# Turning the second norm's tiles of the first two sequences through DRAM instead of on TensorE

## The chip, the cores and the metric

One core of a Trainium2 chip runs the whole program. The metric is device microseconds of one launch, the median of several runs; a profiled execution comes with a trace of every engine.

## The reference

The input `x` holds 4 sequences of 512 tokens, 512 wide. A layer of gated linear attention and a layer of a gated MLP are added to it, each behind a layer norm:

```
x = x + attention(layernorm(x))     # 4 heads of 128, chunks of 128 tokens, a running state per head
x = x + ffn(layernorm(x))           # gate and up 512 -> 4096, gelu(gate)*up, down 4096 -> 512

# attention, per sequence b, chunk n, head h
q, k, v = x@Wq + bq, x@Wk + bk, x@Wv + bv ;  k = k / |k|
cla     = cumsum(log(sigmoid(x@Walpha + balpha) + 1e-6))        # along the chunk
attn    = (q k^T) * beta * exp(cla_i - cla_j), lower triangle
y       = attn v + exp(cla) * (q state) ;  state = state * exp(cla_end) + v^T (k beta exp(cla_end - cla))
```

The MLP's weights are 4-bit codes with a scale for every 32 of them, unpacked on the chip. All is float32; the MLP's products are made of three parts (high, low, middle) of each number.

## The kernel before

The first phase is cut into 48 *places*, `p` from 0 to 47: 12 for each of the four sequences `b`, namely four V products, four Q products and four K products (`product_v`, `product_q`, `product_k`), each one [128 x 512]. The MLP follows, in rounds over weight tiles, and its first rounds are woven into the last places. All instructions are in the order in which the program writes them (a manual schedule): each engine has one queue in that order, and all transfers are issued by SP, on one queue.

`behind(p)` writes what goes behind product `p`. The chunks of attention follow the products at a distance. Chunk `c = 4b + n` (chunk n of sequence b) takes three places:

- place 9 + 3c: `chunk_lead`, `chunk_decay` (`dm` from the row sums `sums`, L608 on ScalarE, L612 on GpSimd);
- place 10 + 3c: `chunk_scores` (scores `sp`, L663; `dm` multiplied by them on VectorE, L674);
- place 11 + 3c: `chunk_sums` (`yp` from `dm`, L717 and L719; added to the residual `xr`, L726; stored as `acc`, L727), and then `second_norm`, the norm that feeds the MLP.

`norm` takes statistics of a tile (L334 to L341) and leaves `settle`, which writes the normalised tile `hn`. There are two ways to turn `hn` so that the model dimension lies on the partitions:

- on TensorE: `hn` goes on the list `turned`, and `turn` transposes it, four 128 x 128 blocks against the identity (L380), into a PSUM bank; `use` reads that bank;
- through DRAM, where `norm` gets a `way`: `settle` writes `hn` in a crossed order of columns (L349, two instructions), `cross` stores the tile (L310, 256 KB) and two places later loads it back in four transfers of 64 KB (L315), and three places after that `turn_blocks` turns its 32 x 32 blocks on VectorE (L326).

In the kernel before, the second way serves the first norm of sequences 1 to 3 (`way_a`, 12 tiles) and some tiles of k (`way_k`, 6 tiles). The first norm's tiles that take it are written at places 11, 14, ..., 32 for sequences 2 and 3; the tiles of sequence 1 earlier. The second norm's 16 tiles (`hn_f`) are turned on TensorE, two places behind their norm. `use` then makes the three parts `hi`, `lo`, `mi` (L406 on ScalarE, L407 and L408 on VectorE) and stores them to DRAM, three transfers of 256 KB (L410, `h<-g`), where the MLP's rounds load them (`x<-h`).

Two lists of postponed work hang on the places: `first_of[p]` is done at the beginning of `behind(p)`, `last_of[p]` at its end. Some loads are tied to places too. `load_sums(b, 0)` (L579), which brings the first chunk's row sums of a sequence from the little table `rows` (L563), is written at place 12b + 7 behind the calls of `turn`, two places ahead of the `chunk_decay` that reads it. Of each further chunk they are loaded three places ahead.

SBUF tiles of 2 KB a partition come from a list of free homes (`one_k`), first in, first out.

Of the kernel before, what the change touches and what calls it, by code (L numbers as in the profile page):

```python
# [21 lines left out]
P = 128  # L22
# [13 lines left out]
def f32(t):  # L36
    return t.bitcast(F32)
# [3 lines left out]
def tile_gated_linear_attention__then__nvfp4_geglu(  # L41
# [19 lines left out]
    nc = tc.nc  # L61
# [15 lines left out]
    h2d = [  # L77
        [dram.tile([KC, P, T], F32, tag=f"h2_{b}_{j}", name=f"h2_{b}_{j}") for j in range(3)]
        for b in range(B)
    ]  # L80
# [40 lines left out]
    one_k = Homes("b", 42, [P, T], two_k)  # L121
# [4 lines left out]
    def heads(t):  # L126
        return t.rearrange("p (h d) -> p h d", d=P)
# [170 lines left out]
    first_of, last_of = {}, {}  # L298
# [5 lines left out]
    def crossed(t):  # L304
        return t.rearrange("p (w k i) -> p k w i", w=KC, i=32)

    def cross(src, key, use, landing, turning):

        way = dram.tile([KC, P, P], F32, tag=f"way_{key}", name=f"way_{key}")
        nc.sync.dma_start(way.rearrange("w p m -> p w m"), f32(src).rearrange("p (w m) -> p w m", m=P))  # L310

        def land():
            t = one_k.get(f"way_{key}")
            for a in range(KC):
                nc.sync.dma_start(f32(t)[:, a * P : (a + 1) * P], way[:, a * 32 : (a + 1) * 32, :])  # L315
            last_of.setdefault(turning, []).append(lambda: use(t))

        first_of.setdefault(landing, []).append(land)

    def turn_blocks(t, *to):  # L320

        new = f32(t).rearrange("p (a k i) -> p k a i", a=KC, i=32)
        done = 0
        for part in to:
            n = part.shape[1]
            nc.vector.transpose(part.rearrange("p k (a j) -> p k a j", j=32), new[:, done : done + n])  # L326
            done += n
        one_k.put(t)

    def norm(src, key, use, parts=1, within=None, way=None):  # L330


        st = small.tile([P, 6], F32, tag="st", name=f"st_{key}")
        nc.vector.bn_stats(st, f32(src))  # L334
        if within:
            within()
        mv = small.tile([P, 2], F32, tag="mv", name=f"mv_{key}")
        nc.vector.bn_aggr(mv, st)
        rs = small.tile([P, 1], F32, tag="rs", name=f"rs_{key}")
        nc.vector.tensor_scalar(rs, mv[:, 1:2], 1e-5, None, ALU.add)  # L340
        nc.gpsimd.tensor_tensor(rs, rs, minus_half[:, :1], ALU.pow)  # L341

        def settle():

            hn = one_k.get(f"hn_{key}")
            w = D // parts
            if way:
                for c in range(2):
                    nc.vector.tensor_scalar(  # L349
                        crossed(f32(hn)).rearrange("p (c two) w i -> p c two w i", c=2)[:, c],  # L350
                        f32(src).rearrange("p (c w i two) -> p c two w i", c=2, w=KC, two=2)[:, c],
                        mv[:, 0:1], rs, ALU.subtract, ALU.mult,
                    )
                one_k.put(src)
                cross(hn, key, way, place[0] + 1, place[0] + 4)
                one_k.put(hn)
                return
            for cols in (slice(i * w, (i + 1) * w) for i in range(parts)):
                nc.vector.tensor_scalar(
                    f32(hn)[:, cols].rearrange("p (c two j) -> p c two j", two=2, j=P),  # L360
                    f32(src)[:, cols].rearrange("p (c j two) -> p c two j", two=2, j=P),
                    mv[:, 0:1], rs, ALU.subtract, ALU.mult,
                )
            one_k.put(src)
            turned.append((hn, key, use))

        settled.append(settle)
# [34 lines left out]
    def second_norm(b, n, src):  # L402
        def use(tp):
            g = [one_k.get(f"g{j}_{b}_{n}") for j in range(3)]
            hi, lo, mi = g
            nc.scalar.activation(hi, tp, AF.Copy, scale=HI)  # L406
            nc.vector.tensor_tensor(lo, tp, f32(hi), ALU.subtract)  # L407
            nc.vector.scalar_tensor_tensor(mi, f32(hi), ONE_E, tp, ALU.mult, ALU.subtract)  # L408
            for j in range(3):
                nc.sync.dma_start(  # L410
                    h2d[b][j][:, :, n * P : (n + 1) * P].rearrange("k p t -> p k t"), heads(f32(g[j]))
                )
            one_k.put(*g)

        norm(src, f"f{b}_{n}", use)


    zs, ss = {}, {}
# [289 lines left out]
    def chunk_sums(b, n):  # L708
        add = state_sums(b, n) if b < B - 1 else None
        old = ch.pop("old")  # L710
        one_k.put(v_sb.pop((b, n)))
        dm, vb = ch.pop("dm"), ch.pop("vb")
        qc = ch.pop("qc", None)
        yp = psum(f"yp_{b}_{n}")
        for h in range(H):
            hs = slice(h * P, (h + 1) * P)
            nc.tensor.matmul(yp[:, hs], f32(dm)[:, hs], f32(vb)[:, hs], start=True, stop=(n == 0))  # L717
            if n > 0:
                nc.tensor.matmul(yp[:, hs], f32(qc)[:, hs], f32(old)[:, hs], start=False, stop=True)  # L719
        one_k.put(dm, vb)  # L720
        if n > 0:
            one_k.put(qc, old)
        a = acc.pop((b, n))

        def sums():
            nc.vector.tensor_tensor(f32(a), f32(a), yp, ALU.add)  # L726
            nc.sync.dma_start(accd[b * NCH + n], f32(a))  # L727

        def rest():
            if n + 1 < NCH:  # L730
                chunk_values(b, n + 1)
            second_norm(b, n, a)
            if add:
                add()

        return sums, rest
# [3 lines left out]
    for b in range(1, B):  # L740
        for n in range(NCH):
            p = 3 * NCH * (b - 1) + 3 * n - 1 if b > 1 else 2 + 3 * max(n - 1, 0)
# [3 lines left out]
    place, met, summed = [0], set(), []  # L746
# [250 lines left out]
    with tc.manual_schedule():  # L997
# [45 lines left out]
        p = 0  # L1043
# [95 lines left out]
```

## Time and profile before

| | |
|---|---|
| median of 3 runs | 1303.22 us (1302.1 to 1303.25) |
| the profiled execution's own time | 1301.6 us |
| its span, first to last instruction | 1299.9 us |
| TensorE (PE) busy | 1288.6 us, 99% |
| VectorE (DVE) busy | 968.1 us, 74% |
| ScalarE (ACT) busy | 452.2 us, 35% |
| GpSimd (POOL) busy | 113.5 us, 9% |
| SP's DMA queue, share of 16 engines | 59.3% |
| granted TensorE clock, mean | 0.998 |

PE is the matmul side of TensorE, PEld its weight loads, SPq the queue on which SP issues transfers. A line of the timeline gives the start in us from the span's start, the time in us, the engine, the source line, the operation, output and inputs by the program's names, and in brackets how long the engine had been idle and what ended that. Names like `way_a` stand for all buffers of that name.

### The profile page before, as it was taken

The numbers are of one execution on the slowest core, as the hardware profiler recorded it, in microseconds if no ns is written. First come the engines' busy times: TensorE is split into PE (matmuls) and PEld (weight loads), VectorE is DVE, ScalarE is ACT, GpSimd is POOL, SyncE is SP. The second block draws the span as 40 slices with busy tenths as digits, with TensorE's granted clock in tenths as the row PEclk, the third lists the DMA queues.
The fourth block names the chain that finished last, engine by engine and source line by source line (L and its number), as shares of the span: only waits on it lengthen the run. The fifth ranks groups of instructions, "written<-read, shape, count | busy, mean of one in ns | idle before, by whom it ended". The sixth has DMA issues, their size and how long they took to land.

```text
span 1299.9 us, 17044 instructions
## 1 busy us (share of the span) xinstructions
PE 1288.6 (99%) x5736; PEld 1030.6 (79%) x5736; DVE 968.1 (74%) x1581; ACT 452.2 (35%) x878; POOL 113.5 (9%) x179
## 2 busy tenths in 40 slices
PE   9999999999999999999999999999999999999998
PEld 6667576778888888888888888888888888887886
DVE  4577865877777777777777777777777777777566
ACT  2333335743333333333333333333333333332332
POOL 1526462400000000000000000000000000000000
PEclk9999999999999999999999999999999999999999
DMA  6556667976565656555555565656555555555473
GB/s 208 163 163 191 196 191 226 310 263 213 179 195 178 194 178 194 178 195 178 194 178 194 178 194 179 195 178 194 179 194 179 192 181 190 182 179 199 167 253 126
DMA packets 195383, 250.24 MB, mean 193 GB/s; under 512 B 16672, under 2 KB 93792, under 8 KB 195296
## 3 DMA queue, kind: packets, MB, share of 16 engines
q1 hardware_dynamic: 195296, 249.16, 59.3%
q8 instruction: 45, 0.74, 0.2%
q14 instruction: 42, 0.34, 0.1%
HBM read 191.91 MB, written 57.18 MB: 192 GB/s over the span
## 4 chain that ended last, share of the span: by engine, by line
PE 95%; DVE 2%; DMA 1%; ACT 1%; issue 0%; SPq 0%; POOL 0%; DVEq 0%; ACTq 0%; POOLq 0%
PE pa L853 35%; PE p_d L897 26%; PE pb L853 18%; PE pq L450 4%; PE pk L474 3%; PE pva L425 2%; PE pvb L432 2%; PE yp L717 1%; PE sp L663 1%; PE yp L719 1%; PE dp L688 1%; PE tp_f L380 0%; DMA sums<-rows 0%; DMA acc<-acc 0%; DMA x<-h 0%
## 5 line engine op out<-in xcount | busy, mean ns | idle before, releaser
L853 PE MATMUL pa<-x,wgu 128*128 128x512 f32 x2048 | 508.5, 390 | 0.1
L853 PEld LDWEIGHTS pa<-x,wgu 128*128 128x128 f32 x2048 | 384.7, 188 | 80.0 <-DVE acc L909 0.4
L897 PE MATMUL p_d<-wd,i 128*128 128x512 f32 x1542 | 357.3, 389 | 2.3 <-DVE xr L726 0.6
L897 PEld LDWEIGHTS p_d<-wd,i 128*128 128x128 f32 x1542 | 288.2, 188 | 65.8 <-DVE i L877 2.1
L858 ACT ACTIVATE t<-pb 128x512 f32<-128x512 f32 x256 | 151.2, 591 | 357.9 <-PE pb L853 354.0
L853 PE MATMUL pb<-x,wgu 128*128 128x512 f32 x1024 | 273.7, 389 | 0.0
L859 DVE TENSOR_TENSOR t<-pa,t 128x512 f32<-128x512 f32 x256 | 176.4, 689 | 81.7 <-ACT t L858 76.4
L853 PEld LDWEIGHTS pb<-x,wgu 128*128 128x128 f32 x1024 | 192.3, 188 | 40.2
L905 DVE SCALAR_TENSOR_TENSOR acc<-p_d,acc 128x512 f32<-128x512 f32 (+1 forms) x137 | 93.3, 681 | 127.4 <-PE p_d L897 124.0
L873 ACT ACTIVATE i<-t 128x512 fp32r<-128x512 f32 x128 | 81.1, 634 | 194.2 <-DVE t L870 191.1
L865 ACT ACTIVATE t<-t 128x512 f32<-128x512 f32 x128 | 81.1, 634 | 136.0 <-DVE t L859 136.0
L877 DVE TENSOR_TENSOR i<-t,i 128x512 fp32r<-128x512 f32 x128 | 88.3, 690 | 26.0 <-ACT i L873 24.2
L909 DVE TENSOR_TENSOR acc<-acc,p_d 128x512 f32<-128x512 f32 x135 | 92.8, 688 | 14.4 <-PE p_d L897 0.5
L870 DVE SCALAR_TENSOR_TENSOR t<-t,t 128x512 f32<-128x512 f32 x128 | 88.6, 692 | 4.3
L928 POOL TENSOR_TENSOR acc<-acc,last 128x512 f32<-128x512 f32 x1 | 1.3, 1295 | 1015.1 <-ACT last L927 1015.1
L878 DVE SCALAR_TENSOR_TENSOR i<-i,t 128x512 fp32r<-128x512 f32 x128 | 88.9, 694 | 0.0
L450 PE MATMUL pq<-hT,wq 128*128 128x512 f32 x128 | 57.6, 595 | 0.0
L474 PE MATMUL pk<-wk,hT 128*128 128x512 f32 x128 | 57.4, 592 | 0.0
L450 PEld LDWEIGHTS pq<-hT,wq 128*128 128x128 f32 x128 | 23.6, 190 | 24.1 <-issue 23.9
L474 PEld LDWEIGHTS pk<-wk,hT 128*128 128x128 f32 x128 | 23.2, 190 | 23.9 <-issue 23.9
L183 DVE TENSOR_TENSOR wgu<-wgu,wgu 128x1024 fp32r<-128x1024 f32 x32 | 38.9, 1215 | 0.0
L180 DVE SCALAR_TENSOR_TENSOR wgu<-wgu,w_gu 128x1024 fp32r<-128x1024 f32 x32 | 38.9, 1215 | 0.0
(120 smaller groups left out, 901.6 us busy)
## 6 DMA issues: line engine op xcount, KB each, us to landing
x<-h SPq DMA_DIRECT2D x420, 256.0 KB
acc<-acc SPq DMA_DIRECT2D x256, 256.0 KB
h<-g SPq DMA_DIRECT2D x48, 256.0 KB
x<-in_x SPq DMA_DIRECT2D x16, 256.0 KB
pk_gu<-in_gate_p SPq DMA_DIRECT2D x32, 128.0 KB
sc_gu<-in_gate_s SPq DMA_DIRECT2D x64, 64.0 KB
pk_gu<-in_up_p SPq DMA_DIRECT2D x32, 128.0 KB
sc_gu<-in_up_s SPq DMA_DIRECT2D x64, 64.0 KB
```

What stands on the lines that cost most here:

```text
L450: nc.tensor.matmul(pq, f32(wq[k // 2])[:, k % 2, h * P : (h + 1) * P], f32(hT[b][k // 2])[:, k % 2, :], start=(k == 0), stop=(k == KC - 1),)
L474: nc.tensor.matmul(pk, f32(hT[b][k // 2])[:, k % 2, n * P : (n + 1) * P], f32(wk[k // 2])[:, k % 2, :], start=(k == 0), stop=(k == KC - 1),)
L853: nc.tensor.matmul(o, w3[j][:, k % 2, c * P : (c + 1) * P], x[j * KC + k], start=(j == js[0] and k == 0), stop=(j == js[-1] and k == KC - 1),)
L858: nc.scalar.activation(f32(t), pb, AF.Copy, scale=-1.0 / ONE_E)
L859: nc.vector.tensor_tensor(f32(t), pa, f32(t), ALU.add)
L865: nc.scalar.activation(f32(g), f32(g), AF.Gelu_apprx_tanh, scale=ONE_E)
L870: nc.vector.scalar_tensor_tensor(f32(u), f32(g), ONE_E, f32(u), ALU.mult, ALU.mult)
L877: nc.vector.tensor_tensor(il, f32(u), f32(ih), ALU.subtract)
L878: nc.vector.scalar_tensor_tensor(im, f32(ih), ONE_E, f32(u), ALU.mult, ALU.subtract)
L897: nc.tensor.matmul(banks[key_][:, part], inter[i][j][:, n * P : (n + 1) * P], wd[ms[i] // 2][j][:, ms[i] % 2, part], start=(i == 0 and j i ...
L905: nc.vector.scalar_tensor_tensor(a, banks[n, False, part.start][:, part], ONE_E, a, ALU.mult, ALU.add)
L909: nc.vector.tensor_tensor(a, a, banks[n, True, 0], ALU.subtract)
```

## The change

Eight of the second norm's 16 tiles, those of sequences 0 and 1, get a `way`: they are stored crossed, loaded back, turned in 32 x 32 blocks on VectorE into a new tile `h2T` in SBUF, and split into `hi`, `lo`, `mi` from there. For tile c that is: store at place 11 + 3c, loads at 13 + 3c, turn and split at the end of place 16 + 3c (it was in the middle of 13 + 3c). The three stores to `h2d` are made at the beginning of place 17 + 3c. Tiles of sequences 2 and 3 stay as they were.

```
@@ -406,13 +406,27 @@
             nc.scalar.activation(hi, tp, AF.Copy, scale=HI)
             nc.vector.tensor_tensor(lo, tp, f32(hi), ALU.subtract)
             nc.vector.scalar_tensor_tensor(mi, f32(hi), ONE_E, tp, ALU.mult, ALU.subtract)
-            for j in range(3):
-                nc.sync.dma_start(
-                    h2d[b][j][:, :, n * P : (n + 1) * P].rearrange("k p t -> p k t"), heads(f32(g[j]))
-                )
-            one_k.put(*g)
-
-        norm(src, f"f{b}_{n}", use)
+
+            def store():
+                for j in range(3):
+                    nc.sync.dma_start(
+                        h2d[b][j][:, :, n * P : (n + 1) * P].rearrange("k p t -> p k t"), heads(f32(g[j]))
+                    )
+                one_k.put(*g)
+
+
+            if b < 2:
+                first_of.setdefault(place[0], []).append(store)
+            else:
+                store()
+
+        def way(t):
+            whole = one_k.get(f"h2T_{b}_{n}")
+            turn_blocks(t, heads(f32(whole)))
+            use(f32(whole))
+            one_k.put(whole)
+
+        norm(src, f"f{b}_{n}", use, way=way if b < 2 else None)
```

## The prediction

> **What bounds the kernel now.** I read the page first, for the engine that is full, then the chain that ended last.
>
> ```profile
> PE 1288.6 (99%) x5736; PEld 1030.6 (79%) x5736; DVE 968.1 (74%) x1581; ACT 452.2 (35%) x878; POOL 113.5 (9%) x179
> PE 95%; DVE 2%; DMA 1%; ACT 1%; issue 0%; SPq 0%; POOL 0%; DVEq 0%; ACTq 0%; POOLq 0%
> ```
>
> TensorE is never idle, so whatever is taken off it is time gained, as long as nothing that it waits for comes late. So next its timeline in the attention phase:
>
> ```profile
> 105.25 0.60 PE L380 MATMUL tp_f<-ident,hn_f 128*128 128x128 f32 x4
> 105.68 1.06 PE L663 MATMUL sp<-q,kT 128*128 128x128 f32 x8
> ...
> 168.87 1.16 PE L717 MATMUL yp<-vb,dm 128*128 128x128 f32 x8 [0.21 <-DVE dm L674]
> ...
> 263.62 0.66 PE L593 MATMUL tpk<-ident,k 128*128 128x128 f32 x4 [2.57 <-DVE acc L905]
> 264.41 3.68 PE L853 MATMUL pa<-x,wgu 128*128 128x512 f32 x8
> ```
>
> The four transposes of a tile take 0.43 us from start to start. Only two waits stand in this phase. At 168.87 `yp` of chunk (2,0), sequence 2's first, waited for `dm`. The gap of 2.57 us was followed by 3.4 us at half clock: the `pa` behind it took 3.68 us where others take 2.0.
>
> The third view is what stands behind that `dm`, on SP, ScalarE and VectorE:
>
> ```profile
> 153.54 2.25 SPq L315 DMA_DIRECT2D way_a<-way_a  x4
> 155.89 2.75 SPq L410 DMA_DIRECT2D h<-g  x3
> 158.73 0.69 SPq L579 DMA_DIRECT2D sums<-rows  x1
> ...
> 163.98 1.28 ACT L608 ACTIVATE dm<-sums,ncla 128x128 f32<-128x128 f32 x4 [3.73 <-DMA sums<-rows]
> ...
> 168.14 0.68 DVE L674 TENSOR_TENSOR dm<-sp,dm 128x512 f32<-128x512 f32 x1
> ```
>
> The chunk's row sums are issued only behind the turned tile's four loads, ScalarE stands 3.73 us for them, and `dm` ends as TensorE wants it. So SP's queue is next to the path. It is late already: the transposes of place 25 ran at 119.25, and that place's `h<-g` were issued at 128.23.
>
> Last, how full the DMA is, with the windows view (the last but one column is the share of 16 engines):
>
> ```profile
> 68.00:69.00 1.00, 1.00 (x11) 1.00 (x11) 0.00 (x0) 0.05 (x1) 0.00 (x0) 1.00 0.30 89
> 70.00:71.00 1.00, 1.00 (x6) 0.84 (x6) 0.93 (x3) 0.00 (x0) 0.00 (x0) 1.00 1.00 288
> 75.00:76.00 1.00, 1.00 (x3) 0.34 (x3) 1.00 (x3) 0.00 (x0) 1.00 (x2) 1.00 0.28 86
> ```
>
> At 68 and at 75 only loads of the turned tiles move: 0.28 to 0.30, some 4.6 engines of 16. The landing events say the same: each 64 KB load lands 0.8 us behind the one before, as long as a whole 256 KB takes (0.65 to 0.77).
>
> **The change, part by part.** *TensorE* loses 8 x 4 transposes: 8 x 0.43 = 3.5 us, all on the path. The Trainium skill (TensorE: Matmul & The Clock Gate, Part 4) gives some 275 ns for a transpose in a kernel; the page's mean is 273 ns. Taken as a cost it would make 8 x 4 x 0.275 = 8.8 us. But they overlap, and the start-to-start rows decide: 3.5 us.
>
> *VectorE*, for each tile: `hn_f` becomes two crossed instructions (L349, 470 ns each) instead of one of 574: +0.37. The turn into `h2T` is +0.70 (the `kT` row of L326). `lo` and `mi` from SBUF cost what they did from PSUM (L877 and L878, 690 and 694, against 689 and 676). +1.07 us in a cycle of three places of 14.4 us, where DVE is busy 10.1 to 12.6 us of 15: cover of 2 us or more. The split now stands behind `dm` and not ahead of it, which takes DVE's waits for `g` (14.6 us in 10) from in front of `dm`: good for TensorE. *ScalarE*: +0.04 us (L873 against L406), and `g` now waits for the turn; behind it nothing waits that TensorE needs soon. Without these covers they would cost 9 us.
>
> *SP* gains a store and four loads for each tile, 0.38 + 4 x 0.56 = 2.6 us of issue, and the three `h<-g` move behind the loads of `x`, `xr` and `sums`, to the next place, ahead of `acc` and of the next tile's store. Nothing soon reads `h2d` (first at place 40; the last store is at 38). But SP goes in order: the loads of `way_f` wait for their store to land (4 to 5 us, as those of `way_a` do now), and queued behind that wait are `way_a`'s loads, `sums`, `x` and `xr`. VectorE waits for the first, ScalarE for the second.
>
> *DMA*. Here a rule speaks against the change. By the bytes, a tile adds 1024 packets of 512 B at 29 ns (mean in this stretch): 1.9 us of 16 engines in 14.4, with a share of 0.61 to 0.74 now. That would be hidden, and the sum would be -3.5. The Trainium skill (DMA: Bandwidth & Descriptors, "Why a DMA increments its semaphore by 16 and not by 1") says that the hardware queues use only the largest k up to 16 that divides both sides' slowest dimension, and on the lowest-numbered k engines. These loads go from [4, 32, 128] to 128 partitions: k = 4, always the same four. The 0.28 above bears it out (a store, 128 against 128, gets 16). So every turned tile queues on four engines, which also carry a sixteenth of all else; their time is what counts: 4 x 0.80 + 0.73 for the store = 3.9 us in each cycle.
>
> How much room is there? Between 60 and 166 us the DMA records leave 8.6 us without traffic; for another 31 us few engines move, the four with a backlog. At the row sums of (2,0), seven tiles have been stored and loaded: 7 x 3.9 = 27.5, less 8.6 if every hole is filled, is 18.9 us late. A hand recurrence agrees. Each transfer lands at the later of issue + 3.05 and the landing before + its service; each issue waits for the eighth before it to land, and for its data. On the order before, it has the loads at 153.54 start at 153.65 and these sums land at 163.05 (163.90 in the trace). On the new order they land at 181.3: +18.3.
>
> From there: 163.9 + 18.3 = 182.2; L608 1.28, L612 0.64, L674 0.68 and three hand-overs of 0.1 make 185.1 for `yp`, against 168.87: +16.2, with the 3.5 already inside, since TensorE comes early and waits. It will have stood idle for many us, so as after the 2.57 us gap it runs 3.4 us at half clock: +1.7. Earlier waits (`v` of (2,3) at place 27 wants `hT`, 2 to 3 us; `dm` about place 31, some 5) are swallowed by this one. Later places catch nothing up: TensorE is full again. Sum +17.9: 1301.6 + 17.9 = 1319.5 for an execution like the profiled one. The median of the runs was 1.6 above it, so I say 1320.
>
> The slack of the turned tiles: before, a `way_a` tile lands 4.6 to 9 us ahead of its turn on VectorE (147.9 against 152.5 at the least).
>
> **Rivals.**
> 1. *The queue is late, but less.* A set issued at 141.25 into a full queue landed within 2.4 us of its first. With 3.1 us for a tile instead of 3.9: 7 x 3.1 - 8.6 = 13.1, so +10.7 and +1.7: 1314. With 2.4, +7: 1309. It belongs to the forecast's case down to about 1311, and to a milder case, 1304 to 1311.
> 2. *The other side: the lateness stays inside the slack*, and only the transposes count: 1301.6 - 3.5 = 1298.1, in the runs' terms 1299 to 1300. Point of decision: six tiles (to place 28) may add 8.6 + 4.6 us, 2.2 us each. For it speaks that every tile is given five places to come back, and the 16-engine share. Against it, that 0.8 us steps of landings would have to halve.
> 3. *The gain is lost on VectorE*: 75 to 90 us is 12.6 of 15 busy, with +1.07 and a wait of 0.8 for `g` in each cycle; a tenth to half a us of wait at each `yp` cancels the 3.5 us: within 2.6 us of no change.
> 4. *Worse*: VectorE, held at `turn_blocks`, writes later `hn` later, so that queue and VectorE wait in turn, and several idle gaps each bring the half clock: 1331 to 1345.
>
> **How the numbers follow.** Forecast's case (1311 to 1331) 0.68; milder 0.12; rival 2 0.08; rival 3 0.05; worse 0.07. The range 1304 to 1331 leaves out rivals 2 to 4, 0.20. Faster by over 0.2% (2.6 us, about what a measurement of this kernel tells from no change): 0.08; within: 0.05; slower: 0.87.
>
> **What would show it.** If right: 32 `tp_f` on PE instead of 64; at `yp` of (2,0) (L717 behind the pair pk, dp) a wait of several us, put down to DVE `dm`; ScalarE's L608 there waiting for `sums<-rows` until 178 to 186; DVE's L326 `h2T` and `hT` waiting for DMA from place 25 on; a dip of the granted clock between 160 and 200 us; from 200 us on, the same work as before, shifted. Wrong, if TensorE has no wait over 1 us before 200 us (rival 2), if its waits there are put down to DVE or PSUM with the DMA landed in time (rival 3), or if two sets of loads in a row land faster than 0.8 us each (rival 1).

## The result, and the profile after

The changed kernel takes 1320.53 us (median of 4 runs, 1319.77 to 1323.21), the kernel before 1302.66 in the same comparison: ratio 1.0144, 95% interval 1.0132 to 1.0156, so slower by 1.4%. The forecast was 1320. The profiled execution has a span of 1319.1 us, before 1299.9.

The page of the changed kernel, the engines' busy times and the chain that ended last:

```profile
PE 1292.9 (98%) x5704; PEld 1031.5 (78%) x5704; DVE 975.5 (74%) x1597; ACT 452.5 (34%) x878; POOL 111.8 (8%) x179
PE 88%; DVE 3%; DMA 3%; SPq 2%; ACT 1%; POOL 1%; issue 1%; DVEq 0%; ACTq 0%; POOLq 0%
```

TensorE has 32 instructions fewer (5704 against 5736), and the chain is no longer TensorE's from end to end: its share fell from 95% to 88%, and DMA, SP and VectorE took the rest. TensorE's busy time rose although its work shrank; in part that is the 9.5 us of it that ran at half clock before 200 us. Its timeline, the instructions behind a wait:

```profile
110.20 1.16 PE L731 MATMUL yp<-vb,dm 128*128 128x128 f32 x8 [0.80 <-DVE dm L688]
134.18 3.89 PE L439 MATMUL pva<-wva,hT 128*128 128x264 f32 x8 [8.28 <-DVE hT L326]
155.86 0.39 PE L574 MATMUL rps<-tri,la 128*16 128x128 f32 x2 [1.02 <-ACT la L556]
162.92 1.13 PE L677 MATMUL sp<-q,kT 128*128 128x128 f32 x8 [2.59 <-DVE kT L326]
184.88 1.16 PE L731 MATMUL yp<-vb,dm 128*128 128x128 f32 x8 [1.39 <-DVE dm L688]
...
214.71 0.49 PE L731 MATMUL yp<-vb,dm 128*128 128x128 f32 x2 [0.58 <-DVE dm L688]
256.05 0.49 PE L867 MATMUL pb<-x,wgu 128*128 128x512 f32 x1 [0.24 <-DMA x<-h]
256.80 1.15 PE L867 MATMUL pb<-x,wgu 128*128 128x512 f32 x2 [0.26 <-DMA x<-h]
```

Where the kernel before had one wait of 0.21 us between 10 and 255 us, there are now waits from 110 us on. The line at 184.88 is the `yp` of chunk (2,0), at 168.87 before: 16.0 us later. The line at 134.18 is the largest wait, and the 3.89 us of its eight matmuls (1.95 elsewhere) are the half clock behind it. The granted clock is the number ahead of the last two in the windows view:

```profile
130.00:140.00 10.00, 5.82 (x14) 4.55 (x15) 7.32 (x20) 3.37 (x7) 1.30 (x3) 0.50 0.58 171
160.00:170.00 10.00, 7.41 (x26) 4.09 (x26) 8.53 (x20) 4.58 (x10) 3.05 (x4) 0.83 0.66 200
180.00:190.00 10.00, 8.61 (x44) 6.48 (x43) 5.17 (x9) 4.32 (x22) 5.20 (x10) 1.00 0.95 303
```

It was at half from 130.1 to 140.3 and from 164.2 to 167.6, and full at 184.88. What stands behind `yp` of (2,0), on ScalarE and VectorE:

```profile
182.11 1.28 ACT L622 ACTIVATE dm<-sums,ncla 128x128 f32<-128x128 f32 x4 [6.59 <-DMA sums<-rows]
```

```profile
184.14 0.69 DVE L688 TENSOR_TENSOR dm<-sp,dm 128x512 f32<-128x512 f32 x1 [5.13 <-POOL dm L626]
```

The row sums landed at 182.03 us by the landing events (163.90 before), ScalarE had stood 6.59 us for them, and the rest of the chain to `yp` took 2.9 us. Behind the large wait is another chain. ScalarE, between 119 and 132 us:

```profile
119.03 0.61 ACT L633 ACTIVATE cd<-sums 128x512 f32<-128x512 f32 x1
131.73 0.63 ACT L406 ACTIVATE g<-h2T 128x512 fp32r<-128x512 f32 x1 [12.08 <-DMA h<-g]
```

and VectorE in the same stretch:

```profile
123.41 0.71 DVE L326 STREAM_TRANSPOSE h2T<-way_f 128x512 f32<-128x512 f32 x1
132.39 0.69 DVE L407 TENSOR_TENSOR g<-h2T,g 128x512 fp32r<-128x512 f32 x1 [8.28 <-ACT g L406]
133.07 0.69 DVE L408 SCALAR_TENSOR_TENSOR g<-g,h2T 128x512 fp32r<-128x512 f32 x1
133.68 0.77 DVE L326 STREAM_TRANSPOSE hT<-way_a 128x256 f32<-128x256 f32 x2
```

The first part of a split (`g`, L406) needed a home that was still being stored by an earlier `h<-g`. That store, issued at 127.04 behind other loads, landed at 131.63. VectorE stood 8.28 us for L406, and behind it stood the turn into `hT`, whose own loads had landed at 125.66. So the 8.28 us that the view puts down to "DVE hT" are a late transfer too, of another tile.

The windows view while the loads of turned tiles move:

```profile
101.00:102.00 1.00, 1.00 (x4) 0.50 (x3) 0.95 (x3) 0.43 (x1) 0.92 (x3) 1.00 0.24 67
102.00:103.00 1.00, 1.00 (x4) 0.45 (x3) 1.00 (x2) 0.00 (x0) 0.92 (x3) 1.00 0.29 82
103.00:104.00 1.00, 1.00 (x3) 0.38 (x2) 0.52 (x1) 0.00 (x0) 0.92 (x2) 1.00 0.33 95
```

Loads are queued all the time here, and a quarter to a third of the engines works. The landing events say the same. A store of `way_f` leaves 16 of them on its semaphore, and each of the 32 loads of `way_f` leaves five: an early one, about 1 us behind the issue in 31 of the 32, and four at the end. With the share of about a quarter, that says that four engines carry a load. Loads of turned tiles that are issued in a row land 0.83 us apart (median), so they wait for the same engines; which of the 16 these are, no run shows.

### The profile page after: what moved, and what is told of

It reads as the page before. It is cut to its first block, busy times and chain, and to the rows that moved or that the text cites. A ratio compares the mean times of both kernels' runs of the same rounds, so it can differ in the third digit from the quotient of the medians.

```text
span 1319.1 us, 17051 instructions
## 1 busy us (share of the span) xinstructions
PE 1292.9 (98%) x5704; PEld 1031.5 (78%) x5704; DVE 975.5 (74%) x1597; ACT 452.5 (34%) x878; POOL 111.8 (8%) x179
## 4 chain that ended last, share of the span: by engine, by line
PE 88%; DVE 3%; DMA 3%; SPq 2%; ACT 1%; POOL 1%; issue 1%; DVEq 0%; ACTq 0%; POOLq 0%
PE pa L867 34%; PE p_d L911 25%; PE pb L867 17%; PE pk L488 3%; PE pq L464 3%; PE pva L439 1%; PE pvb L446 1%; DMA h<-g 1%; DMA x<-h 1%; PE sp L677 1%; PE yp L731 1%; SPq L315 1%; PE yp L733 0%; SPq L412 0%; DMA acc<-acc 0%
## 5 line engine op out<-in xcount | busy, mean ns | idle before, releaser
L439 PE MATMUL pva<-wva,hT 128*128 128x264 f32 x128 | 33.2, 405 | 8.6 <-DVE hT L326 8.3
```

## The experiments

My theory: the added loads use four of the 16 DMA engines, 0.8 us for each 64 KB, and fill the queue until everything on it is late. Rivals: SP, which stands at each store before it can issue the loads and all behind them; the order of the work on VectorE; the postponed stores, which hold homes; and the mere bytes. Times are medians; the kernel before is at 1302.3 to 1302.4 in all of these comparisons.

**The parts alone.** The transfers without their use, and the use without the transfers.

```
# transfers only (cut: the stores h<-g are made at once, and def way is gone)
-norm(src, f"f{b}_{n}", use, way=way if b < 2 else None)
+norm(src, f"f{b}_{n}", use, copy=b < 2)
...
+if copy:
+    cross(hn, key, one_k.put, place[0] + 1, place[0] + 4)
 turned.append((hn, key, use))

# no transfers
+if key[0] == "f":
+    last_of.setdefault(place[0] + 4, []).append(lambda: way(hn))
+    return
 cross(hn, key, way, place[0] + 1, place[0] + 4)
```

> The transfers of the change alone: the eight tiles are stored and loaded back in the same places, but what comes back is not used; the tiles are turned on TensorE, split and stored to h2d where the kernel before does it. Theory 'the transfers make the loss': sums of (2,0) land at 178 to 184 us, yp of (2,0) at 181 to 188 us; the 3.5 us of transposes are swallowed by TensorE's waits: 1316 to 1324 us. Rival 'VectorE, or the later split and stores of h': 1301 to 1305 us.

Measured: 1326.37 us, ratio 1.0173 (1.0150 to 1.0196). Row sums of (2,0) landed at 187.5 us. TensorE's timeline:

```profile
117.56 2.07 PE L724 MATMUL yp<-vb,dm 128*128 128x128 f32 x8 [5.92 <-DVE dm L681]
168.78 0.80 PE L724 MATMUL yp<-vb,dm 128*128 128x128 f32 x2 [5.66 <-DVE dm L681]
192.46 2.08 PE L724 MATMUL yp<-vb,dm 128*128 128x128 f32 x8 [6.35 <-DVE dm L681]
```

The transfers alone make the loss, and more: every wait between 40 and 280 us is now at `yp`. All three ranges were missed at the top: the sums by 3.5 us, `yp` of (2,0), the last line, by 4.5 and the time by 2. I had let the waits swallow the transposes' 3.5 us; the median is 5.8 above the whole change's.

> The change without its transfers: neither the store nor the four loads of the eight tiles are made; VectorE turns the blocks of hn itself, at the same place, and splits, and the stores to h2d come at the place that follows. The 32 x 32 blocks are then not in their right places in h2d: that part of the computation is left out. Theory: what is left is the gain, 8 x 0.43 = 3.5 us, with VectorE's added 1.07 us a tile under cover: 1297 to 1300 us, and no wait of TensorE over 0.5 us before 200 us. Rival 'VectorE': over 1303 us, with waits at yp put down to dm.

Measured: 1301.55 us, ratio 0.9989 (0.9977 to 1.0001), 12 runs from 1298.68 to 1305.26. The loss is gone without the transfers, but so is most of the gain: 1301.55 is 1.55 above my range, 0.84 below the kernel before and not clear of noise. The profiled execution shows three things that eat it up, told by how late each matmul is against the same one of the kernel before. Its first `pva`, at 7.36 us, long ahead of the first changed tile, ran 3.89 us where that of the kernel before took 2.05; by 14 us TensorE was 2.1 late. Between 225 and 239 us it lost another 1.1, where `pb` waited for `x<-h`. The third is on VectorE:

```profile
149.99 1.13 PE L680 MATMUL sp<-q,kT 128*128 128x128 f32 x8 [1.25 <-DVE kT L326]
```

This wait is over my 0.5. So VectorE's added work is not wholly under cover, but the price is of a us, not of ten. Whether the other executions lost the rest in the same places is not shown.

**The four engines.** The same four loads, bytes and packets, cut so that each fills 32 partitions with four pieces; first for the second norm's tiles alone, then for all tiles that go through DRAM, then the latter in the kernel before.

```
-for a in range(KC):
-    nc.sync.dma_start(f32(t)[:, a * P : (a + 1) * P], way[:, a * 32 : (a + 1) * 32, :])
+for w in range(KC):
+    nc.sync.dma_start(f32(t)[w * 32 : (w + 1) * 32, :].rearrange("i (a m) -> i a m", m=P),
+                      way[w].rearrange("(a i) m -> i a m", i=32))
```

> The other cut of the loads for every tile that goes through DRAM: the eight of the second norm, the 12 of the first and the six of k. Theory 'four engines': the queue has more room than before the change, so the whole of the 3.5 us is kept: 1297 to 1300 us. Rivals 'SP's order' and 'bytes': 1315 us or more.

Measured: 1299.41 us, ratio 0.9974 (0.9966 to 0.9982): the change is now a gain. The windows view of this kernel, while such loads move:

```profile
68.00:69.00 1.00, 1.00 (x11) 1.00 (x10) 0.00 (x0) 0.76 (x2) 0.00 (x0) 1.00 0.49 144
127.00:128.00 1.00, 1.00 (x7) 0.87 (x6) 0.96 (x4) 0.99 (x3) 0.54 (x1) 1.00 0.46 131
```

The share is 0.46 to 0.49 where it was 0.24 to 0.33. Each load now leaves 16 landing events in place of five, and loads issued in a row land 0.28 us apart (median), not 0.83; SP issues one in some 0.47 us here, so the engines stand for part of the time. TensorE has no wait between 40 and 252 us, and the page reads

```profile
PE 1285.2 (99%) x5704; PEld 1027.5 (79%) x5704; DVE 976.0 (75%) x1597; ACT 452.7 (35%) x878; POOL 113.5 (9%) x179
PE 96%; DVE 2%; DMA 1%; SPq 1%; ACT 1%; issue 0%; POOL 0%; DVEq 0%; ACTq 0%
```

`yp` of (3,1) in the kernel before and in this one:

```profile
238.39 0.38 PE L717 MATMUL yp<-vb,dm 128*128 128x128 f32 x2
234.97 0.38 PE L734 MATMUL yp<-vb,dm 128*128 128x128 f32 x2
```

That is 3.42 us earlier, about the 8 x 0.43 of the sum: 0.5 us was lost before 30 us, and the wait of 0.21 is gone too. "Bytes" and "SP's order" as causes by themselves fall: this kernel moves the same bytes in the same order. The cut also takes 0.1 us of SP's time from each load; no run parts this from the engines, but in the changed kernel loads landed 0.83 us apart where SP took 0.52 to issue one, so there SP was not what held them.

> The kernel before, with the other cut of the loads for its 18 tiles that go through DRAM. It tells what the cut is worth without the change. TensorE waited for transfers only once there, 0.21 us: 1301.5 to 1303 us if the cut is worth nothing by itself; 1299 to 1300 us if the 3 us won in the kernel with the cut for all tiles came from the cut and not from the transposes.

Measured: 1301.73 us, ratio 0.9996 (0.9988 to 1.0005). The cut by itself is worth nothing that can be told, so the 3 us belong to the change: the transposes.

> The four loads of a second norm's tile are cut another way: each fills 32 partitions with four pieces of 512 B, where it filled 128 partitions with one piece. Bytes, packets, number of loads and their places are the same; the slowest dimension is 32 on both sides and not 4 against 128. Theory 'four engines': the four loads together then take about what one 256 KB transfer takes, 0.7 to 1.0 us in place of 3.3; a tile adds 1.4 to 1.8 us to the queue, seven add 10 to 12.5 against 8.6 us of room and 4.6 us of slack: no wait at yp of (2,0) over 0.5 us, 1299 to 1304 us. Rival 'SP's order' (the sums and loads stand behind the wait for the store to land, however fast the loads are): 1317 to 1322 us. Rival 'bytes': 1318 to 1322.

Measured: 1313.09 us, ratio 1.0071 (1.0050 to 1.0092): 7 us of the loss gone, 11 left, so 1299 to 1304 was missed by 9. TensorE's waits:

```profile
130.57 3.88 PE L446 MATMUL pva<-wva,hT 128*128 128x264 f32 x8 [5.29 <-DVE hT L333]
157.27 1.13 PE L684 MATMUL sp<-q,kT 128*128 128x128 f32 x8 [2.58 <-DVE kT L333]
```

I had counted 8.6 us of room in the queue over 60 to 166 us. Counted again in the DMA records of the kernel before, as stretches without any packet, it is 7.4, and only 4.1 of it lie before 120 us, while the first four tiles add 4 x 1.6 = 6.4 by then (the store's 0.73 and 0.9 for the four loads). The queue is still nearly full (3.7 us without a packet over 60 to 166 us, against 1.6 in the changed kernel), now with the first norm's and k's loads, which are on four engines as before. Cutting these too took the loss away.

**SP standing at the stores.** In the kernel just shown, SP stood 14.4 us between 60 and 166 us for the stores of `way_f`. One place later they have landed:

```
-cross(hn, key, way, place[0] + 1, place[0] + 4)
+cross(hn, key, way, place[0] + 2, place[0] + 4)
```

> The loads of the stored tiles of both norms stand one place later in SP's order (the place behind the store but one), cut by columns as in the change: still on four engines, 0.8 us each. In SP's order they come behind x, xr and sums of the place before, and their store has long landed when SP reaches them, so SP doesn't stand there with the queue running empty. Theory 'four engines alone': seven tiles still add 27 us to the queue: 1312 to 1321 us. Theory 'four engines, and SP standing at the store': the empty stretches of 3 to 4 us in each cycle go: 1300 to 1309 us.

Measured: 1320.09 us, ratio 1.0138 (1.0122 to 1.0155). Between 60 and 166 us, SP's waits for stores of `way_f` fell from 11.5 us in five (in the changed kernel) to 1.6 in one, and the time is that of the change. So SP's stand at the stores is not what costs the time. Its timeline, for one tile of the changed kernel:

```profile
93.93 0.76 SPq L577 DMA_DIRECT2D rows<-rows  x1
97.24 2.25 SPq L315 DMA_DIRECT2D way_f<-way_f  x4
```

and for another tile, with the loads one place later:

```profile
133.96 1.08 SPq L315 DMA_DIRECT2D way_k<-way_k  x2
135.49 3.55 SPq L315 DMA_DIRECT2D way_f<-way_f  x4
```

In the first, SP stands from 94.7 to 97.24 and then issues four loads in 2.25 us. In the second it hardly stands, but the four take 3.55 us: each issue itself takes 0.74 to 1.15 us, about the pace of 0.8 us at which the loads land. That they wait there for a place in the queue is my reading; no run shows it by itself.

> Both: the loads of both norms one place later, and those of the second norm cut by 32 partitions (16 engines). Theory 'four engines, and SP standing at the store': neither is left for the added tiles: 1298 to 1301 us, and no wait of TensorE over 0.5 us before 200 us. If the loss of the kernel with the other cut alone (1313 us) came from elsewhere, from VectorE say, it stays: 1308 to 1313 us.

Measured: 1309.79 us, ratio 1.0055 (1.0040 to 1.0070). The interval overlaps that of the kernel with the cut alone, so the later place is worth 3 us or nothing. The larger part of what was left, 7.5 of 10.8 us, did not come from SP's stand.

**The order on VectorE, and the stores.** `hT` turned ahead of the split that it stood behind, in the change and in the kernel with the cut for the second norm; and the stores not postponed.

```
-last_of.setdefault(turning, []).append(lambda: use(t))
+todo = last_of.setdefault(turning, [])
+todo.insert(0 if key[0] == "a" else len(todo), lambda: use(t))
```

> The change with one order swapped: at a place where both come due, the first norm's tile is turned into hT ahead of the turn and split of the second norm's tile. In the changed kernel hT of (2,3) stood on VectorE for 8.3 us behind a split whose first part waited on ScalarE for a free home (h<-g still on its way), with its own loads landed 8 us before; pva of (2,3) waited 8.28 us. Theory 'the full queue sets the pace': that wait falls under 2 us, others take its place later (sums of (2,0) still land at 179 to 183 us), 1316 to 1321 us. Theory 'the hand-over on VectorE makes the loss': 1307 to 1313 us.

Measured: 1320.51 us, ratio 1.0148 (1.0122 to 1.0173). TensorE's timeline:

```profile
126.12 2.05 PE L440 MATMUL pva<-wva,hT 128*128 128x264 f32 x8 [0.69 <-DVE hT L327]
141.29 2.04 PE L678 MATMUL sp<-q,kT 128*128 128x128 f32 x8 [7.96 <-DVE kT L327]
...
184.34 1.75 PE L732 MATMUL yp<-vb,dm 128*128 128x128 f32 x8 [2.85 <-DVE dm L689]
```

The wait of 8.28 fell to 0.69, and one of 7.96 came up 15 us later, at the next thing on VectorE. Row sums of (2,0) landed at 181.5, `yp` ran at 184.34. Behind the 7.96 is the same thing as before: VectorE stood 5.23 us for `g`, until 132.2, and the turn into `kT` came late. What the waits are put down to is interchangeable; the queue sets the pace.

> The same swap on the kernel whose second norm's tiles are loaded by 32 partitions (1313 us). There the queue is less full, and the wait of pva of (2,3) for hT was 5.3 us. If what was left of the loss came from hT behind the waiting split: 1300 to 1306 us. If the queue, still slowed by the loads of the other tiles on four engines, sets it: 1310 to 1314 us, with a wait at sp or yp instead.

Measured: 1312.69 us, ratio 1.0083 (1.0060 to 1.0105): unchanged as well, with 5.35 us at the same `sp`.

```
-if b < 2:
-    first_of.setdefault(place[0], []).append(store)
-else:
-    store()
+store()
```

> The change with one part undone: the three stores h<-g are made directly behind the split, not at the beginning of the place that follows. They then stand ahead of the next loads on SP, and the homes come free earlier. Theory 'the four engines': no less traffic, 1316 to 1323 us. Theory 'the postponed stores hold the homes': 1305 to 1312 us.

Measured: 1320.28 us, ratio 1.0137 (1.0115 to 1.0158). The postponement costs nothing and saves nothing.

**How many tiles.** `b < 1` for `b < 2` in both lines of the diff; and, with the cut for all tiles, `4 * b + n < 10`.

> The change for sequence 0 alone: four tiles through DRAM, the other twelve on TensorE. Theory 'the queue adds up': the same recurrence as for the prediction has sums of (2,0) land some 10 us later than in the kernel before (7 of 18 for the four tiles by themselves, the rest from SP standing at stores), yp of (2,0) at 175 to 179 us, and 1308 to 1314 us. Rival 'a threshold that eight tiles pass and four do not': 1300 to 1303 us.

Measured: 1317.25 us, ratio 1.0114 (1.0099 to 1.0129). The first four tiles make 15 of the 18 us, above my range. TensorE's waits came early:

```profile
112.27 1.82 PE L731 MATMUL yp<-vb,dm 128*128 128x128 f32 x8 [2.92 <-DVE dm L688]
140.31 3.51 PE L439 MATMUL pva<-wva,hT 128*128 128x264 f32 x8 [10.19 <-DVE hT L326]
```

That is 13.1 us by 141 us. `yp` of (2,0) ran at 184.67, above my 175 to 179 as well. Four tiles add 4 x 3.9 = 15.6 us to the queue, and 4.1 us of room before 120 us leaves 11.5. The recurrence behind my range took each store's data to be ready when they were in the kernel before, and gave some 10. That the later tiles cost so little beside (3.3 us more, while they save 1.7) fits room that comes late, and TensorE's own waits give the queue more of it; no run measured that room by itself.

> The kernel with the other cut of the loads for all tiles (1299.4 us), and ten of the second norm's tiles through DRAM in place of eight. With the queue not in the way two tiles are worth 0.87 us: 1298 to 1299 us. If the room ends there, a wait of TensorE shows between 170 and 210 us and it is 1300 us or more.

Measured: 1302.37 us, ratio 0.9999 (0.9990 to 1.0008). The two further tiles lose what the eight had won. Until 207 us they pay: TensorE is 4.35 us ahead of the kernel before, where it was 3.45 ahead with eight tiles. Then it waits, and VectorE shows for what:

```profile
209.60 0.49 PE L734 MATMUL yp<-vb,dm 128*128 128x128 f32 x2 [1.96 <-DVE dm L691]
```

```profile
208.25 0.69 DVE L411 SCALAR_TENSOR_TENSOR g<-g,tp_f 128x512 fp32r<-128x512 f32 x1 [3.44 <-DMA h<-g]
208.86 0.69 DVE L691 TENSOR_TENSOR dm<-sp,dm 128x512 f32<-128x512 f32 x1
```

`dm` stood behind a split whose third part waited 3.44 us for a home. The store that held the home was issued at 203.27, behind six loads of `x<-h` for the MLP, and landed at 208.23. It is the route of the change's largest wait again, in a queue that is now filled by loads on 16 engines. Of the 4.35 us, 2.5 went here and the rest, and more, between 233 and 242 us, where `pb` waited for `x<-h` and the clock fell to half; why these loads came late stays open. The kernel with eight tiles and the cut for all is the best one seen.

## Why the prediction was right

*The four engines, 0.8 us a load.* Right, and shown: with the loads of all tiles cut otherwise, and nothing else, 1320.5 became 1299.4, and that cut alone was worth nothing. A load leaves four landing events behind the early one in one cut, and 16 in the other. The rule of the Trainium skill (DMA: Bandwidth & Descriptors, "Why a DMA increments its semaphore by 16 and not by 1") on the largest k up to 16 that divides both sides' slowest dimension says the same: 4 against 128 gives four, 32 on both sides gives 16.

*The row sums.* Forecast to land at 182.2, landed at 182.03; `yp` of (2,0) at 185.1, ran at 184.88. The recurrence on the new order was right. That the short sum, 27.5 less 8.6, gave nearly the same was luck, for two errors in it met. Up to these sums the kernel before had 7.3 us without a packet and the changed one still 2.5, so 4.8 us were filled and not 8.6. And 15 stores `h<-g` are issued ahead of these sums in place of 21, since they come later in the change; at the 0.65 to 0.77 us of a 256 KB transfer that takes some 4.3 us off (an estimate). 27.5 - 4.8 - 4.3 = 18.4, and 18.1 was measured.

*TensorE's 3.5 us.* Right: 3.42 in the kernel where nothing covers them, 0.107 us for each of 32. The Trainium skill's 275 ns (TensorE: Matmul & The Clock Gate, Part 4) agrees with what one takes in the profile, 273 ns, and not with what its removal saves.

*VectorE.* Its busy time rose by 7.4 us (8 x 1.07 = 8.6 forecast). It is covered in the best kernel; one wait of 1.25 us in the kernel without transfers shows how near its end the cover is.

*The earlier waits.* Wrong in size: "2 to 3 us" at `v` of (2,3), measured 8.28. The term that failed is the room: 8.6 us were set against seven tiles as one sum, though the first four tiles find only 4.1 of it. The same term missed the kernel with four tiles and the one with the cut for the second norm alone. It missed the route too: `hT` waited behind a split for a free home, not for its own loads. The forecast had TensorE reach `yp` of (2,0) early and wait there for many us. In fact it was 15.3 us late by 167.7 us, and the wait at that `yp` was 1.39. The end was unharmed, since whichever wait comes first, TensorE can run that `yp` only when the row sums are there.

*The half clock.* Wrong in place. The long gaps, and the half clock behind them, came at 134 and 164 us, ahead of (2,0), where the row sums covered them; at 184.88 TensorE had waited 1.39 us and ran at full clock. Nor was the rest only shifted. In place of the 1.7 us, 3.4 were lost after it: `yp` of (3,2) is 19.4 us late (270.61 against 251.20) where that of (2,0) is 16.0, by the small waits from 208 to 257 us and the slow starts behind them. The two profiled executions lie 19.2 us apart and the medians 17.9. So it was luck that the sum, 17.9, met the medians to a tenth: a term in it was another's, and the executions of the changed kernel alone scatter by 3.4 us.

*Rivals.* The slack did not absorb the lateness, and VectorE was no bound by itself. The milder case wanted landings faster than 0.8 us, and they were not. Even with an estimated 1.6 us a tile, in the cut for the second norm alone, the time was 1313 and not in the milder case's 1304 to 1311: again the room.

## What to carry to other kernels

Count a transfer by the engines that it can use, not by its bytes: a share of 0.3 in the windows view while loads are queued says that a transfer with the same bytes and another cut may be faster, here by three times; here the count of its landing events told how many engines it had. Work that is taken off an engine and given to a queue is paid for there, so make the transfer cheap first and move the work then. And set added traffic against the room that lies before the point where it is needed, not against the room of the phase.

## What the runs showed that I had not expected

- A 64 KB load of `way_f` on a free queue landed 2.95 to 3.15 us after its issue in the first cut and 1.75 to 1.9 us in the other, and SP took 0.52 us to issue the one and 0.42 the other (medians over the 32 loads of `way_f`).
- With a full queue the waits of TensorE can be moved from place to place by reordering (8.28 us at `pva`, then 7.96 at `sp`) without a change of the time: 1320.53 and 1320.51.
- Moving the loads behind the landing of their store took most of SP's waits there away (11.5 us to 1.6), and left the time within the interval.
